# A mask added to attention scores by blocks of the identity: sixteen 32 by 32 products in place of four of 128 by 128

## The chip, the cores and the metric

The kernel runs on one core of one Trainium2 chip. The metric is the device time of one execution, in microseconds. A core has a matrix engine (TensorE, "PE" in the profile; its loading of the stationary operand stands apart as "PEld"), three engines for element-wise work (VectorE, "DVE"; ScalarE, "ACT"; GpSimd, "POOL"), and a queue engine that issues transfers ("SP"). Each engine works through its own instructions in order, and they wait for each other by semaphores.

## The reference: what is computed

One decoder layer over 128 sequences of 128 rows and 256 columns: self-attention, cross-attention against a context of the same size, and a feed-forward part with ternary weights, each behind a layer norm and added to its input. Attention has 16 heads of 16 columns. What the change touches is the mask in cross-attention:

```python
scores = jnp.einsum('bhqd,bhkd->bhqk', Q, K) / jnp.sqrt(jnp.float32(D_K))
scores = jnp.where(mask == 0, jnp.float32(1e-09), scores)
attn = jax.nn.softmax(scores, axis=-1)
```

One mask of 128 by 128 (query by key) serves all sequences and heads. A masked score is set to 1e-9, not to minus infinity.

## The kernel before

**Groups and steps.** Sequences are handled four at a time, in 32 groups. One step of attention is one sequence of one stage, all 16 heads. A period has eight steps: four of self-attention of a group and four of cross-attention of the group before it. So there are 128 steps of each stage.

**A step's scores are computed twice.** `maxima` forms scores with a query on each partition, only to find every row's largest value; `transposed_scores` forms them again with a key on each partition, which is what the later product with the values needs, and the maxima are brought in there. In `maxima`, four strips of 32 rows of the array work side by side (r = 0 to 3). The tiles s[0] and s[1] have two banks of PSUM each (a bank is 512 float32 per partition), so strip r has one bank, s[r // 2][:, r % 2], with four heads of 128 keys. In cross-attention the mask is added first: `ident_b`, the identity in bfloat16, times `never`, which is -1e30 where the mask is 0 and 0 elsewhere, repeated for four heads. That is one product per bank, over the whole 128 by 128 array (line 543). The products of queries and keys (line 554) then add to it. VectorE takes the maxima (`mx`, line 565).

**What frees what.** All score tiles, `s` and `st`, share four banks, so the first products of `maxima` wait until ScalarE's two exponentials (line 645) have read the step before. The transposed maxima `pn` (line 581) and the attention outputs `av` (line 657) share one more bank: `av` waits until `pn` has been read. In self-attention VectorE reads it for `q_max` (line 586); in cross-attention ScalarE reads it for `first` (line 596), and then VectorE reads both for `negm_t` (line 598).

**The order of a step**, as `attention` writes it by hand: the maxima of the following step; the outputs of the step before; the transposed scores of this step; the transposed maxima of the following one; in cross-attention, the weights of this step. Between these parts a string of letters, `ORDER`, says which piece of other work is put in: preparing self-attention (n), keys of the context (k), preparing cross-attention (c) and finishing a group with its feed-forward part (f). Nothing reorders the instructions later.

**The setup.** Before the first step the weights are loaded, one transfer after the other on SP's queue (line 153), then the mask (line 188). Two products per attention (line 177) take the value bias through the output weights. The mask is compared with 0 (`masked`, line 191) and scaled (`never`, line 193). Then comes the layer norm of the first group (lines 211 to 222), and its queries, keys and values, and then the ternary weights (lines 454 to 478), which load `raw` over the same queue.

**Buffers by tag.** Tiles of the pool `p_one` with one tag share one buffer. The tag `g_0` holds `bv_cols` of the setup, then `below`, and later a part of the feed-forward; `xn_0` and `xn_1` hold `unmasked` and `masked` in the setup.

The lines that the rest speaks of:

```python
    ident_b = const.tile([P, P], BF16, name="ident_b")
    nc.vector.tensor_copy(ident_b, ident)
...
            for r in range(S4):
                nc.tensor.matmul(
                    s[r // 2][:, r % 2],
                    ident_b,
                    never[:, None, :].to_broadcast([P, 4, P]),
                    start=True,
```

Of the kernel before, what the change touches and what calls it, by code (L numbers as in the profile page):

```python
# [18 lines left out]
F32 = mybir.dt.float32  # L19
F32R = mybir.dt.float32r  # L20
BF16 = mybir.dt.bfloat16
I32 = mybir.dt.int32
AF = mybir.ActivationFunctionType
ALU = mybir.AluOpType
AX = mybir.AxisListType
PSUM = bass.MemoryType.PSUM

P = 128
# [9 lines left out]
S4 = 4  # L38
# [3 lines left out]
NEVER = -1e30  # L42
# [17 lines left out]
def tile_decoder_layer(ctx: ExitStack, tc: tile.TileContext, a: dict, out: bass.AP):  # L60
    nc = tc.nc
    n_groups = a["x"].shape[0] // G

    const = ctx.enter_context(tc.tile_pool(name="const", bufs=1))
    p_in = ctx.enter_context(tc.tile_pool(name="p_in", bufs=5))
    p_act = ctx.enter_context(tc.tile_pool(name="p_act", bufs=2))
    p_one = ctx.enter_context(tc.tile_pool(name="p_one", bufs=1))
    p_att = ctx.enter_context(tc.tile_pool(name="p_att", bufs=2))
# [22 lines left out]

    ident = const.tile([P, P], F32, name="ident")
    make_identity(nc, ident)
    ident_b = const.tile([P, P], BF16, name="ident_b")
    nc.vector.tensor_copy(ident_b, ident)
    minus_half = const.tile([P, 1], F32, name="minus_half")
    nc.gpsimd.memset(minus_half, -0.5)
    masked_score = const.tile([P, 1], F32, name="masked_score")
# [7 lines left out]
        nc.vector.tensor_reduce(parity[:, e : e + 1], ident_heads[:, e], AX.XY, ALU.add)  # L106

    ident_strips = ident.rearrange("p (s r) -> p s r", s=S4)

# [2 lines left out]
    for n in range(4):  # L114
        for i in range(2):
            rows = ident_strips[:, :, 4 * i + n]
# [72 lines left out]

    masked = p_one.tile([P, P], F32, name="masked", tag="xn_1")  # L190
    nc.vector.tensor_scalar(masked, unmasked, 0.0, None, ALU.is_equal)
    never = const.tile([P, P], BF16, name="never")
    nc.vector.tensor_scalar(never, masked, NEVER, None, ALU.mult)

    least = const.tile([P, 1], F32, name="least")
    nc.vector.tensor_reduce(least, masked, AX.X, ALU.max)
# [336 lines left out]
    def score_tiles(name):  # L533
        return [ps_s.tile([P, 2, 4, P], F32, name=name, tag="s") for _ in range(2)]

    def maxima(stage, b, j):

        qt, kt = ready[stage, b]["q"], ready[stage, b]["k"]
        tok = slice(j * P, (j + 1) * P)
        s = score_tiles("s")  # L540
        if stage == "cross":
            for r in range(S4):
                nc.tensor.matmul(  # L543
                    s[r // 2][:, r % 2],
                    ident_b,
                    never[:, None, :].to_broadcast([P, 4, P]),
                    start=True,
                    stop=False,
                    skip_group_check=True,
                )  # L550
        for o in range(CC):
            for r in range(S4):
                strip = slice(r * 32, (r + 1) * 32)
                nc.tensor.matmul(  # L554
                    s[r // 2][:, r % 2, 2 * o : 2 * o + 2],
                    qt[strip, o, tok],
                    kt[strip, o, :, tok],
                    start=(stage == "self"),
                    stop=True,
                    skip_group_check=True,  # L560
                )

        mx = p_stat.tile([P, S4, 4, 2], F32, name="mx", tag="mx")[:, :, :, 0]
        for half in range(2):
            nc.vector.tensor_reduce(  # L565
                mx[:, 2 * half : 2 * half + 2], s[half], AX.X, ALU.max, negate=True
            )
        negm = negms[stage]
        if stage == "cross":
            twice = mx[:, :, None, :].to_broadcast([P, S4, 2, 4])  # L570
            nc.vector.tensor_scalar(negm[:, :, 0:2], twice, least, None, ALU.min)
        else:
            halves = negm.rearrange("p s a b -> p s (a b)").rearrange("p s (h d) -> p s h d", d=HD)
            heads = mx.rearrange("p s (o e) -> p s o e", e=2)
            for e in range(2):
                nc.vector.tensor_copy(halves[:, :, 1 - e, 0:CC], heads[:, :, :, e])
        return negm

    def transposed_maxima(stage, b, j, negm):
        pn = ps_av.tile([P, 4, P], F32, name="pn", tag="av")[:, 3]  # L580
        nc.tensor.transpose(pn, negm.rearrange("p s k n -> p (s k n)"), ident)  # L581
        if stage == "self":
            qt = ready[stage, b]["q"][:, :, j * P : (j + 1) * P]
            q_max = p_att.tile([P, CC, 2, P], F32, name="q_max", tag="q_max", bufs=1)
            for e in range(2):
                nc.vector.scalar_tensor_tensor(  # L586
                    q_max[:, :, e],
                    pn[:, None, :].to_broadcast([P, CC, P]),
                    max_rows[:, e : e + 1],
                    qt,  # L590
                    ALU.mult,
                    ALU.add,
                )
            return q_max
        first = p_att.tile([P, P], F32R, name="first", tag="first", bufs=1)
        nc.scalar.copy(first, pn)
        negm_t = p_att.tile([P, P], F32R, name="negm_t", tag="negm_t")
        nc.vector.scalar_tensor_tensor(
            negm_t, first.bitcast(F32), minus_second, pn, ALU.mult, ALU.add
        )  # L600
        return negm_t
# [70 lines left out]
    def attention():  # L672
        w_t = added = None
        for i in range(-1, 2 * G * (n_groups + 1) + 1):
            here, following, before = row(i), row(i + 1), row(i - 1)
            cross = i % (2 * G) >= G
            if following:
                negm = maxima(*following)
            if i >= 0:
                yield  # L680
            if before:
                outputs(*before, w_t)
            if i >= 0:
                yield
            if here:
                s = transposed_scores(*here, added)
                if not cross:
                    w_t = weights(here[0], s, None)
            if i >= 0:
                yield  # L690
            added_here = added
            if following:
                added = transposed_maxima(*following, negm)
            if i >= 0:
                yield
            if cross and i >= 0:
                if here:
                    w_t = weights(here[0], s, added_here)
                yield
# [76 lines left out]
```

## Time and profile before

| | |
|---|---|
| median of three runs | 2883.38 us (2882.04 to 2885.99) |
| the profiled execution | 2880.45 us, of it a span of 2878.4 us |
| granted clock of TensorE, mean over the span | 0.982 |
| scores for the maxima (line 554), TensorE busy | 299.0 us, 4096 records |
| outputs (line 657), TensorE busy | 279.1 us, 8192 records |
| maxima (line 565), VectorE | 512 of 1214 ns |
| exponentials (line 645), ScalarE | 512 of 1022 ns |

A float32 product leaves two records, one for each of its passes; bfloat16 and the rounded float32 form leave one. A record of TensorE gives the start of a product and a modelled end, which includes the time through the pipe, so consecutive products overlap in it; the start-to-start distance is what a product costs. The chain of waits goes back from the last instruction, at each step to what released it or to the instruction before it on its engine; its shares are shares of the span. In the groups, a name and an arrow read "written from read".

### The profile page before, as it was taken

The numbers are of one execution on the slowest core, as the hardware profiler recorded it, in microseconds if no ns is written. First come the engines' busy times: TensorE is split into PE (matmuls) and PEld (weight loads), VectorE is DVE, ScalarE is ACT, GpSimd is POOL, SyncE is SP. The second block draws the span as 40 slices with busy tenths as digits, with TensorE's granted clock in tenths as the row PEclk, the third lists the DMA queues.
The fourth block names the chain that finished last, engine by engine and source line by source line (L and its number), as shares of the span: only waits on it lengthen the run. The fifth ranks groups of instructions, "written<-read, shape, count | busy, mean of one in ns | idle before, by whom it ended". The sixth has DMA issues, their size and how long they took to land.

```text
span 2878.4 us, 73779 instructions
## 1 busy us (share of the span) xinstructions
PE 2768.6 (96%) x31261; PEld 1984.6 (69%) x31261; DVE 2048.5 (71%) x3787; ACT 1547.9 (54%) x2369; POOL 1373.5 (48%) x1425
## 2 busy tenths in 40 slices
PE   4789999999999999999999999999999999999985
PEld 2456777777777777777777767777777777777664
DVE  4467777777777777777777877777777777777663
ACT  0345555555555556555556555555655555555443
POOL 1324545454454545454455545454544545454343
PEclk8899999999999999999999999999999999999997
DMA  2111221121122122122112112211211221211101
GB/s 78 31 39 40 55 55 32 47 55 37 49 55 52 30 53 48 39 54 54 33 46 55 40 47 54 55 32 47 55 39 47 55 47 36 51 47 34 45 24 31
DMA packets 110359, 130.92 MB, mean 45 GB/s; under 512 B 32592, under 2 KB 68816, under 8 KB 110032
## 3 DMA queue, kind: packets, MB, share of 16 engines
q1 hardware_dynamic: 110032, 126.22, 17.8%
q8 instruction: 247, 4.05, 0.6%
q14 instruction: 80, 0.66, 0.1%
HBM read 71.65 MB, written 18.87 MB: 31 GB/s over the span
## 4 chain that ended last, share of the span: by engine, by line
PE 93%; DVE 3%; DMA 1%; POOL 1%; ACT 1%; issue 1%; SPq 0%; POOLq 0%; ACTq 0%; DVEq 0%
PE st L612 10%; PE s L554 10%; PE av L657 9%; PE py L431 9%; PE po L272 8%; PE ph L379 8%; PE pv L272 8%; PE pk L260 8%; PE pq L260 8%; PE pg L408 4%; PE s L543 4%; PE pt L240 3%; PE st L636 3%; PE pn L581 1%; DVE mx L565 1%; DVE st L622 1%
## 5 line engine op out<-in xcount | busy, mean ns | idle before, releaser
L565 DVE TENSOR_REDUCE mx<-s 128x8 f32<-128x1024 f32 x512 | 600.5, 1214 | 103.4 <-PE s L554 103.3
L217 POOL TENSOR_SCALAR rstd<-agg 128x4 f32<-128x4 f32 (+1 forms) x160 | 38.4, 240 | 1214.7 <-DVE agg L212 1214.7
L645 ACT ACTIVATE w_t<-st 128x1024 f32<-128x1024 f32 x512 | 496.4, 1022 | 225.0 <-PE st L612 196.8
L222 POOL TENSOR_SCALAR xn<-x,agg,rstd 128x256 f32<-128x256 f32 x384 | 465.5, 1225 | 10.0
L622 DVE COPY_PREDICATED_SCALAR st<-masked_t,masked_score 128x1024 f32 x256 | 315.7, 1279 | 85.4 <-PE st L612 82.6
L416 ACT ACTIVATE g<-pg,ln_w 128x256 fp32r<-128x256 f32 x512 | 211.9, 477 | 215.8 <-PE pg L408 212.6
L660 ACT COPY raw<-av 128x512 f32<-128x512 f32 x256 | 150.2, 587 | 318.8 <-PE av L657 318.5
L554 PE MATMUL s<-kt,qt 32*128 32x256 f32 x4096 | 299.0, 404 | 1.7 <-ACT w_t L645 1.7
L350 POOL TENSOR_TENSOR o_raw<-o_raw,factors 128x256 f32<-128x256 f32 x256 | 179.2, 728 | 243.0 <-DMA factors<-by_head 193.8
L657 PEld LDWEIGHTS av<-w_t,v 128*32 128x32 f32 x8192 | 209.7, 110 | 111.2 <-issue 44.8
L657 PE MATMUL av<-w_t,v 128*32 128x128 f32 x8192 | 279.1, 277 | 3.4 <-ACT w_t L645 1.2
L554 PEld LDWEIGHTS s<-kt,qt 32*128 32x128 f32 x4096 | 187.9, 186 | 132.9 <-issue 83.7
L222 POOL TENSOR_SCALAR g<-g,agg,rstd 128x1024 f32<-128x1024 f32 x64 | 276.3, 4317 | 6.7
L379 PE MATMUL ph<-w_fc,xn 128*128 128x512 f32 x1024 | 273.3, 409 | 1.2 <-ACT g L386 1.2
L431 PE MATMUL py<-w_proj,g 128*128 128x256 f32 x2048 | 271.2, 288 | 0.3 <-DVE g L418 0.3
L431 PEld LDWEIGHTS py<-w_proj,g 128*128 128x128 f32 x2048 | 254.2, 193 | 14.4 <-issue 9.6
L418 DVE SCALAR_TENSOR_TENSOR g<-pg,ln_w,g 128x256 fp32r<-128x256 f32 x512 | 216.7, 475 | 33.3 <-ACT g L416 29.8
L379 PEld LDWEIGHTS ph<-w_fc,xn 128*128 128x128 f32 x1024 | 188.0, 191 | 54.3 <-issue 16.4
L308 DVE COPY v<-pv 128x512 f32<-128x512 f32 x128 | 86.3, 674 | 147.6 <-PE pv L272 147.5
L586 DVE SCALAR_TENSOR_TENSOR q_max<-pn,max_rows,qt 128x256 f32<-128x256 f32 x256 | 110.5, 473 | 110.7 <-PE pn L581 110.7
L386 ACT ACTIVATE g<-ph 128x512 f32<-128x512 f32 x256 | 146.3, 597 | 78.9 <-PE ph L379 78.2
L354 DVE TENSOR_TENSOR x<-x,po 128x512 f32<-128x512 f32 x128 | 87.5, 683 | 110.2 <-PE po L272 110.2
(112 smaller groups left out, 4829.8 us busy)
## 6 DMA issues: line engine op xcount, KB each, us to landing
o_raw<-raw SPq DMA_DIRECT2D x512, 64.0 KB
factors<-by_head SPq DMA_DIRECT2D x128, 256.0 KB
x<-in_x_dram SPq DMA_DIRECT2D x32, 512.0 KB
ctx_t<-in_ctx_t_dram SPq DMA_DIRECT2D x32, 512.0 KB
out_dram<-x SPq DMA_DIRECT2D x32, 512.0 KB
sums<-raw SPq DMA_DIRECT2D x128, 16.0 KB
by_head<-r SPq DMA_DIRECT2D x64, 32.0 KB
raw<-in_w_fc_t_dram SPq DMA_DIRECT2D x1, 1024.0 KB
```

Source lines behind the costliest of these rows:

```text
L222: engine.tensor_scalar(dst[:, j], src[:, j], agg[:, j, 0:1], rstd[:, j : j + 1], ALU.subtract, ALU.mult)
L260: nc.tensor.matmul(out, w[:, c, o * P : (o + 1) * P], src_t[:, c], start=(c == 0), stop=(c == CC - 1))
L272: nc.tensor.matmul(rows[:, j], src_t[:, c, (j0 + j) * P : (j0 + j + 1) * P], w[:, c], start=(c == 0), stop=(c == CC - 1),)
L379: nc.tensor.matmul(ph, xn_parts[i][:, c, (j0 + j) * P : (j0 + j + 1) * P], w_fc[:, c, n * 512 : (n + 1) * 512], start=((i, c) == terms[0]) ...
L418: nc.vector.scalar_tensor_tensor(parts[1][:, f0 + f], pieces[:, f], scales[f], parts[0][:, f0 + f].bitcast(F32), ALU.mult, ALU.subtract,)
L431: nc.tensor.matmul(rows[:, j], parts[i][:, f, j * P : (j + 1) * P], w_proj[:, f], start=((i, f) == terms[0]), stop=((i, f) == terms[-1]),)
L554: nc.tensor.matmul(s[r // 2][:, r % 2, 2 * o : 2 * o + 2], qt[strip, o, tok], kt[strip, o, :, tok], start=(stage == "self"), stop=True, sk ...
L565: nc.vector.tensor_reduce(mx[:, 2 * half : 2 * half + 2], s[half], AX.X, ALU.max, negate=True)
L612: nc.tensor.matmul(s[r // 2][:, r % 2, n], kt[strip, n // 2, n % 2, tok], added[strip, n // 2, n % 2] if stage == "self" else qt[strip, n ...
L622: nc.vector.copy_predicated(s[half].rearrange("p r n q -> p (r n) q"), masked_t[:, None, :].to_broadcast([P, 8, P]), masked_score[:, :, No ...
L645: nc.scalar.activation(w_t[:, 2 * half : 2 * half + 2], s[half], AF.Exp)
L657: nc.tensor.matmul(av[32 * r : 32 * r + 32, n], v[:, j, head : head + 32], w_t[:, r, n], start=True, stop=True)
```

## The change

The mask is added by products of 32 by 32 blocks. The array's strip r and column group c take rows 32c to 32c + 31 of the queries for the four heads of bank r: the stationary operand is a 32 by 32 identity on the partitions of strip r, the moving operand is rows 32c to 32c + 31 of the mask, on those same partitions. So `ident_b` shrinks to four identities one below the other, and `never` becomes, on each strip, all 128 rows of the mask in four pieces of 32 rows. Four transfers lay the mask out that way in the setup (`rows`). The tile `first` takes the tag, and so the buffer, of `q_max`.

```diff
-    ident_b = const.tile([P, P], BF16, name="ident_b")
-    nc.vector.tensor_copy(ident_b, ident)
...
     ident_strips = ident.rearrange("p (s r) -> p s r", s=S4)
+    ident_32 = p_one.tile([P, 32], F32, name="ident_32", tag="g_0")
+    nc.vector.tensor_reduce(ident_32, ident_strips.rearrange("p s r -> p r s"), AX.X, ALU.add)
+    ident_b = const.tile([P, 32], BF16, name="ident_b")
+    nc.vector.tensor_copy(ident_b, ident_32)
...
-    never = const.tile([P, P], BF16, name="never")
-    nc.vector.tensor_scalar(never, masked, NEVER, None, ALU.mult)
+
+    rows = p_one.tile([P, S4, P], I32, name="rows", tag="g_0")
+    for r in range(S4):
+        nc.sync.dma_start(rows[r * 32 : (r + 1) * 32], a["mask"].rearrange("(c i) k -> i c k", c=S4))
+    never = const.tile([P, S4, P], BF16, name="never")
+    nc.vector.tensor_scalar(never, rows, 0.0, NEVER, ALU.is_equal, ALU.mult)
...
-            for r in range(S4):
-                nc.tensor.matmul(
-                    s[r // 2][:, r % 2],
-                    ident_b,
-                    never[:, None, :].to_broadcast([P, 4, P]),
-                    start=True,
-                    stop=False,
-                    skip_group_check=True,
-                )
+            for c in range(S4):
+                for r in range(S4):
+                    strip = slice(r * 32, (r + 1) * 32)
+                    nc.tensor.matmul(
+                        s[r // 2][c * 32 : (c + 1) * 32, r % 2],
+                        ident_b[strip],
+                        never[strip, c, None, :].to_broadcast([32, 4, P]),
+                        start=True,
+                        stop=False,
+                        skip_group_check=True,
+                    )
...
-        first = p_att.tile([P, P], F32R, name="first", tag="first", bufs=1)
+        first = p_att.tile([P, P], F32R, name="first", tag="q_max", bufs=1)
```

In the changed kernel the mask products are on line 551, the scores on 562, the transposed scores on 620 and the outputs on 665.

## The prediction

> **What bounds the kernel now.** I read the page first (busy shares, then the chain that ended last), then the groups by line and shape, then the chain over one period of 84.6 us in mid-run, then the timeline around the changed products, and last the chain of the first 70 us.
>
> ```profile
> span 2878.4 us, 73779 instructions
> ...
> PE 2768.6 (96%) x31261; PEld 1984.6 (69%) x31261; DVE 2048.5 (71%) x3787; ACT 1547.9 (54%) x2369; POOL 1373.5 (48%) x1425
> ...
> PE 93%; DVE 3%; DMA 1%; POOL 1%; ACT 1%; issue 1%; SPq 0%; POOLq 0%; ACTq 0%; DVEq 0%
> ...
> L543 PE MATMUL s<-never,ident_b 128*128 128x512 bf16 x512 | 133.9, 383 | 1.7 <-ACT w_t L645 1.6
> ```
>
> TensorE carries 93% of the chain, and the next engine is busy 71%. The changed line has 512 products, four in each of 128 steps of cross-attention. Their 133.9 us busy counts the pipe's tail, so I take the chain's pieces instead:
>
> ```profile
> 1412.09 0.11 PE pn L581
> 1412.20 0.86 PE s L543 x4
> 1413.06 1.08 PE s L554 x16
> 1414.13 1.01 PE av L657 x32
> ```
>
> Four products cost 0.86 us, 216 ns each, with nothing beside them. 128 times 0.864 is 110.6 us, 3.8% of the span. Now the starts inside (start, length, engine, line, what):
>
> ```profile
> 1412.03 1.03 PE L543 MATMUL s<-never,ident_b 128*128 128x512 bf16 x4
> 1412.73 0.87 DVE L586 SCALAR_TENSOR_TENSOR q_max<-pn,max_rows,qt 128x256 f32<-128x256 f32 x2
> 1412.99 0.74 PEld L554 LDWEIGHTS s<-kt,qt 32*128 32x128 f32 x16 [0.42 <-issue]
> ...
> 1412.68 0.38 PE L543 MATMUL s<-never,ident_b 128*128 128x512 bf16 x1
> ...
> 1413.74 0.39 PE L554 MATMUL s<-kt,qt 32*128 32x256 f32 x4
> ...
> 1414.06 0.14 PEld L657 LDWEIGHTS av<-w_t,v 128*32 128x32 f32 x5 [0.33 <-issue]
> ```
>
> The fourth product starts at 1412.68 and streams 0.213; the first load of the next form follows at 1412.99, 0.095 after the stream's end. The same 0.09 to 0.10 stands at every change of tile form I looked at. The four row-tiled products of one round (L554) finish within 0.39 of the first start though each takes 0.374: they start about 6.6 ns apart and run at once. The five column-tiled loads of L657 do so too: four 7 ns apart, the fifth, and with it the first product, 28 ns after the first load.
>
> **What the Trainium skill says.** "TensorE: Matmul & The Clock Gate", Part 3, measured speedup: sixteen 32 by 32 tiles with 512 columns ran 10.6 times as fast as one after the other, and a pack takes one product plus some 4 ns per further tile. The trace agrees for four row tiles and for four column tiles (3.3 to 6.6 ns apart); no line of it uses sixteen. That page's pack took 660 ns, so one product there took about 600 against 379 here: it says nothing on whether the faster stream is kept. "TensorEngine Tiling (Array Packing)", Key Properties: changing the tile form drains the array; here that is the 0.095. The same page, Gotcha 1: row tiles that run at once must write different banks. The new code gives strip r bank r, as L554 does.
>
> **The change part by part.**
>
> *Removed:* 0.864 us per step.
>
> *Added in its place, per step.* What stands before the four products is a 128 by 128 form in all 128 steps (63 after pn, the rest after lines 379, 260, 272 and 240), so today no drain stands there; the new form needs one: 0.095. The first load of 32 columns: 0.028, from L657 (for float32; bf16 cannot be much dearer). Sixteen starts: 15 gaps of 3.3 ns (L636, one pass) to 6.6 ns (L554), so 0.05 to 0.10, taken 0.075. The last stream: 0.213, as today. Sum 0.411. The drain ahead of L554 is there before and after. Saved: 0.864 - 0.411 = 0.453 us, between 0.43 and 0.48 by the gaps; times 128 = 58.0 us.
>
> *Can the instructions be fed?* 32 instructions stand where 8 did. Semaphore records of TensorE's sequencer stand 105 ns apart when adjacent and 165 with four products between, so one product costs it 15 ns and 32 some 0.5 us. In all 128 steps its last own wait before the mask products is over at least 1.8 us before they start, so I price this at nothing; if that lead were gone, the gaps would grow to some 30 ns and the step to 0.79.
>
> *First wait that takes some back.* The first and third old products wait for the two exponentials that free the score banks. With strips innermost, the third product comes not 0.43 after the first but 0.01.
>
> ```profile
> 1008.45 1.02 ACT L645 ACTIVATE w_t<-st 128x1024 f32<-128x1024 f32 x1
> ...
> 1009.21 1.03 PE L543 MATMUL s<-never,ident_b 128*128 128x512 bf16 x4
> ```
>
> Here the second exponential ends at 1009.47, 0.26 after the first product's start, plus 0.04 to wake (what waiting products show). The new third product would be ready at 0.095 + 0.028 + 0.01 = 0.13: it waits 0.17 to 0.18, and everything on TensorE's queue behind it too (the other tiles, L554, av). I compared all 128 steps: 30 look like this one (one per period), five near the ends are later still by some 0.3; in the rest the second exponential is over. 30 x 0.18 + 5 x 0.3 = 6.9 us back.
>
> *Second.* Once per period pn of a self step stands right ahead of the mask products, and av (L657) right behind the scores. av's bank is pn's, and q_max frees it. Above, q_max ends at 1413.60 and av's first load starts at 1414.06, 0.46 later; such a hand-over takes about 0.16 (an av that waits starts 0.106 after its semaphore record, which takes 0.05 after the update). So 0.30 is to spare, and 0.453 is wanted: 0.15 x 31 = 4.7 us back. q_max itself waits for VectorE's copy of v, not for the scores, so it doesn't come earlier. The other three av of a period, the transposed scores behind mx, and line 636 behind the predicated copy have either more to spare or move along with the scores; I allow 1 us for them.
>
> *Prologue.* never, today on 128 x 128 behind masked, now reads rows, which four new DMAs fill; they stand on SP between the mask's load and the load of w_fc (SP's issues, then the chain).
>
> ```profile
> 12.56 1.58 SPq L188 DMA_DIRECT2D unmasked<-in_mask_dram  x1
> 15.82 0.37 SPq L454 DMA_DIRECT2D raw<-in_w_fc_t_dram  x1
> ...
> 13.72 2.09 PE pb L177 x4
> ...
> 16.43 0.23 DVE never L193
> ...
> 17.48 0.35 DVE stats L211
> ...
> 21.19 4.86 POOL xn L222 x4
> 26.09 1.33 PE pt L240 x5
> ```
>
> rows takes the buffer that a product of pb frees, as the w_fc load at 15.82 does (its buffer by the other product): the first issue falls between 14.9 and 15.8, the fourth three issue slots of 0.51 later, at 16.4 to 17.4. From issue to use took 2.6 us for the first sums, and at most 3.6 for the mask itself; I take 2.0 to 3.5. So never starts at 18.4 to 20.9 instead of 16.43, and lasts some 0.35 longer for four times the elements (by line 222 on VectorE, 0.82 for 1024). least and stats stand behind it on VectorE, and xn, the transposes and the first projections behind stats: 2.3 to 4.8 us, taken 3.5, all on the chain. w_fc's load comes four slots (2 us) later, but is read only at 40.8. ident_32, its sum and its small copy lie in VectorE's wait of 1.97 us for the first biases.
>
> *At nothing:* first now shares q_max's buffer. first is written after pn, which TensorE runs after the last scores that read q_max; q_max is written by VectorE after the operation that reads first. Neither gains a wait; if one did, it would be at two of eight steps. One semaphore record more on ScalarE and two on VectorE are all that the program shows.
>
> *Sum:* -58.0 + 6.9 + 4.7 + 1.0 + 3.5 = -41.9 us. The profiled execution took 2880.45 (span 2878.4 and 2.05 around it), so 2838.6; the median of the runs is 2883.38, 2.9 higher, so 2841.5, as I forecast: 2842.
>
> **The rivals.**
>
> *A. The tiles run together, but at half the stream rate.* For: sixteen tiles[...] write four banks in each column group; L554 and L657 are float32 at half that rate, and L636, the one-pass row-tiled line, starts a round only every 0.11 us, though its stream of 128 columns would take 0.053. Against: those rounds are as long as a load of 128 columns (0.107), which explains them. Then 0.213 becomes 0.427, a step 0.625, saved 30.6; the exponential's wait stays, q_max's falls away: -30.6 + 6.9 + 3.5 = -20.2, so 2863.
>
> *B. Only four tiles run at once: slower.* No line has tiles of one strip and different column groups in flight on different data together with other strips. If the next group of four waits for the strip, the place is L551 itself: 0.095 + 0.028 + 4 x 0.216 = 0.987, 0.123 more per step, 15.7 in all; with 6.9 and 3.5 it is +26, so 2909. It decides once starts and streams together last over 0.66 us, just over three rounds. Against it: the skill's 10.6, and the overlapping loads and products of L657.
>
> *C. The gain turns into waits.* VectorE's 71% are dense where four steps follow each other. If, beside q_max, the other three hand-overs of a period fell short by about as much (0.15 x 96 = 14 us), the result would be 2856. Against: the idle time that TensorE shows before av now is small.
>
> *D. The change does something else:* excluded; the program has sixteen loads and sixteen products on sixteen tile positions per step.
>
> **How the numbers follow.** My forecast 0.70, A 0.14, B 0.09, C 0.07. Its own range is 2833 (gaps of 3.3 ns, short prologue, half of the waits) to 2852. The range of 2830 to 2868 takes in C and A and leaves out B and the tails. About 0.2% (5.8 us) is what a measurement can tell. Faster: all of the first, A and C but a few hundredths: 0.88; same: 0.03; slower: B, 0.09.
>
> **What would show it.** Right: sixteen products of L551 start within 0.1 us of each other; the piece on the chain is about 0.4 us with the drain, and L562 starts 0.31 after the last start; idle time before L551 by w_t of 5 to 8 us, before av by q_max of about 5; stats starts near 21 us. Wrong: last starts 0.43 apart from the next form's load plus 0.095 (A), starts in four groups 0.2 apart (B), idle time before av in all steps (C), or a prologue that is later by more than 5 us.

## The result, and the profile after

| | before | after |
|---|---|---|
| median of five runs each | 2885.99 us | 2839.25 us |
| lowest to highest | 2882.04 to 2887.87 | 2837.91 to 2845.54 |
| ratio after to before | | 0.9844, 95% interval 0.983 to 0.9859 |

The ratio stands for 45 us, between 41 and 49; the two medians are 46.7 apart. The forecast took 41.9 us off the median then known, 2883.38, which gave 2842.

The profiled execution of the changed kernel was the slowest of its five, 2845.54 us; the one shown of before, 2880.45, was below all five of its runs in the table. So these two executions are only 35 us apart. The page (span; busy time by engine; chain by engine and line) and the group of the changed line (operation, shapes, count; busy us and mean ns; idle time before):

```profile
span 2843.5 us, 76860 instructions
...
PE 2723.7 (96%) x32797; PEld 1965.4 (69%) x32797; DVE 2045.6 (72%) x3788; ACT 1546.9 (54%) x2369; POOL 1371.8 (48%) x1425
...
PE 93%; DVE 3%; DMA 1%; POOL 1%; issue 1%; ACT 1%; SPq 0%; POOLq 0%; ACTq 0%; DVEq 0%
```

```profile
L551 PE MATMUL s<-never,ident_b 32*32 32x512 bf16 x2048 | 64.8, 388 | 2.8 <-ACT w_t L653 2.7
```

The bound is what it was: TensorE has 93% of the chain. 2048 products stand where 512 stood, each as long in the records (388 ns against 383), and together they are busy for 64.8 us instead of 133.9. That is only possible if they lie beside each other. The chain of the changed kernel through the first two cross steps of a period in mid-run (start, us, engine, what, line, records):

```profile
1398.32 0.11 PE pn L589
1398.43 0.36 PE s L551 x16
1398.80 1.15 PE s L562 x16
1399.94 0.04 issue
1399.98 1.08 PE av L665 x32
...
1406.87 0.11 PE pn L589
1406.98 0.36 PE s L551 x16
1407.34 1.08 PE s L562 x16
1408.42 1.91 PE pq L266 x4
1410.33 1.01 PE av L665 x32
1411.35 1.24 PE st L620 x30
```

The mask now takes 0.36 us where it took 0.86. Three places give some of it back. In the first step the scores and av take 1.15 and 1.08 with 0.04 between, where 1.08 and 1.01 stood: av waits. In the second step the transposed scores take 1.24 where they took 1.10. This is that step in the chain of before:

```profile
1421.07 0.86 PE s L543 x4
1421.93 1.07 PE s L554 x16
...
1425.93 1.10 PE st L612 x32
```

And in the third cross step the mask itself takes longer. There the timeline of the changed kernel has this (start, length of the run of records, engine, line):

```profile
1417.02 1.02 ACT L653 ACTIVATE w_t<-st 128x1024 f32<-128x1024 f32 x1
...
1417.88 0.64 PE L551 MATMUL s<-never,ident_b 32*32 32x512 bf16 x16
```

The exponential ends at 1418.04, 0.16 after the first product; the sixteen take 0.64 with their tails here against 0.43 in the other steps, because the third of them starts 0.21 us after the first and not 0.007. So the saving of 4 x 0.50 us per period became 1.43: from the first mask product of a group to that of the next it was 84.61 us before and is 83.18, within 0.02 us in every period of the middle. The 31 distances from the first group to the last add up to 43.0 us less (2601.0 and 2558.0).

Ahead of that, the first mask product came 7.3 us later than in the profile of before, 2.8 of it by the first scores (71.2 against 68.4 us). The first experiment looks at this.

### The profile page after: what moved, and what is told of

It reads as the page before. It is cut to its first block, busy times and chain, and to the rows that moved or that the text cites. A ratio compares the mean times of both kernels' runs of the same rounds, so it can differ in the third digit from the quotient of the medians.

```text
span 2843.5 us, 76860 instructions
## 1 busy us (share of the span) xinstructions
PE 2723.7 (96%) x32797; PEld 1965.4 (69%) x32797; DVE 2045.6 (72%) x3788; ACT 1546.9 (54%) x2369; POOL 1371.8 (48%) x1425
## 4 chain that ended last, share of the span: by engine, by line
PE 93%; DVE 3%; DMA 1%; POOL 1%; issue 1%; ACT 1%; SPq 0%; POOLq 0%; ACTq 0%; DVEq 0%
PE st L620 10%; PE s L562 10%; PE av L665 9%; PE py L437 9%; PE po L278 9%; PE ph L385 8%; PE pv L278 8%; PE pq L266 8%; PE pk L266 8%; PE pg L414 4%; PE pt L246 3%; PE st L644 3%; PE s L551 2%; PE pn L589 1%; DVE mx L573 1%
```

## The experiments

"Period" is the median distance between the first mask products of two groups. All times stand beside runs of the kernel before on the same chip, whose medians were 2885.2 to 2886.3 us.

**1. The changed kernel again.**

> The changed kernel once more, beside the runs of the others. In its first profile the steady period lasted 83.18 us against 84.61 before (1.43 less, 44 us in 31 periods), but the first mask product came 7.3 us later than before, 2.8 of it in the setup and 4.5 in the filling that follows, where one transfer of factors took 6.7 us instead of 3.7 and the clock was low longer. Theory: the 4.5 us are chance of that execution. Then a second profile has the same 83.18 us period, and the first mask product 2 to 4 us later than before. Rival: the change itself delays the filling; then the 7 us return. Time: 2836 to 2846.

Measured: 2840.31 us (2839.82 to 2845.43), ratio 0.9851 (0.9836 to 0.9865); period 83.17; the first statistics at 21.0 us, the first scores at 70.7 and the first mask product at 157.5, 5.5 later than in the first profile of before. The period repeats to 0.01 us. But the first mask product came later than the theory's 2 to 4 us, and earlier than the rival's 7, so this run alone does not decide. All thirteen profiles tell more. Here is the filling, the stretch from the first scores to the first mask product, beside the mean granted clock of TensorE over it:

| filling, us | mean granted clock | kernels |
|---|---|---|
| 83.2 to 84.1 | 0.84 to 0.85 | before, runs 3 and 4 |
| 85.2 to 85.5 | 0.81 | runs 10 and 11 |
| 86.8 to 88.2 | 0.80 to 0.83 | the changed kernel, runs 1, 2, 5, 6, 7 and 8 |
| 90.7 | 0.77 | run 9 |

On the whole the filling is longer where the granted clock was lower. Kernels with the old setup (before, runs 5, 10 and 11) and with the new one have both short and long fillings, so a longer filling is not shown to come from the change. But three of the four with the old setup are in the upper two rows and only two of the nine with the new one, so it is not excluded either: why the clock differed from one execution to the next is not shown.

**2. never filled later.**

```diff
-    rows = p_one.tile([P, S4, P], I32, name="rows", tag="g_0")
-    for r in range(S4):
-        nc.sync.dma_start(rows[r * 32 : (r + 1) * 32], a["mask"].rearrange("(c i) k -> i c k", c=S4))
...
-    nc.vector.tensor_scalar(never, rows, 0.0, NEVER, ALU.is_equal, ALU.mult)
...
     run_now(ternary_weights())
+    rows = p_one.tile([P, S4, P], I32, name="rows", tag="g_0")
...
+    nc.vector.tensor_scalar(never, rows, 0.0, NEVER, ALU.is_equal, ALU.mult)
```

> The changed kernel with the four transfers of rows and never moved behind the ternary weights. Theory: VectorE's wait for rows holds up the layer norm of the first group by 2.6 us, and that is the whole cost of the setup. Then the first statistics start at 17.5 us as before and not at 20.0, the first scores at 68.5 instead of 71.3, and the time is 2 to 3 us lower than the changed kernel's. Rival: the setup is held up by the queue's four more issues, wherever they stand; then the first scores still come after 70 us, and the time stays.

Measured: 2841.46 us (2838.76 to 2844.32), ratio 0.9848 (0.9831 to 0.9865); first statistics at 18.3, first scores at 69.4, first mask product at 157.4. Both starts moved forward, by 1.7 and 1.8 us against the first profile and 2.7 and 1.3 against the second; but the time is the same within its spread, and the first mask product came at the same time too. So the wait for rows holds up the setup by some 2 us, near the 2.6 expected; that this counts in the time is not shown.

**3. The mask added twice.** The second set adds to the first, so the mask's value is doubled and the output unchanged by it.

```diff
-            for c in range(S4):
+            for again, c in [(0, c) for c in range(S4)] + [(1, c) for c in range(S4)]:
...
-                        start=True,
+                        start=not again,
```

> The changed kernel with the sixteen mask products made twice, the second time added to the first (the mask's value doubles, masked scores are still far below every other). Theory: sixteen products that run at once cost one stream of 0.213 us and a few ns each, so a second set costs 0.22 to 0.24 us per step, 28 to 31 us in all, less what the steps that wait for an exponential hide (30 of them 0.21 at most): 22 to 31 us over the changed kernel. Rival 1, the feed of instructions is what a set costs (32 instructions of 15 ns): 0.48 per step, 55 to 62 us. Rival 2, half of the stream rate: 0.43 per step, 50 to 55 us.

Measured: 2860.5 us (2856.93 to 2864.11), 20 over the run beside it. The same first step, from the chain of this kernel:

```profile
1403.17 0.11 PE pn L589
1403.28 0.58 PE s L551 x32
1403.86 1.08 PE s L562 x16
1404.94 1.01 PE av L665 x32
```

A second set costs 0.58 - 0.36 = 0.22 us: one stream. Its first product starts 0.226 after the first set's first, the sixteen again within 0.05. Both rivals fall. And the period grew by 0.51, not by 4 x 0.22: scores and av are back at 1.08 and 1.01 here with no gap. The two hand-overs that the short mask left waiting (0.18 and 0.14 per period) absorb most of the difference. The expectation lacked these two. It let the steps that wait for an exponential hide a part instead, and they hide nothing: in the third cross step too the second set adds 0.22. Hence 20 and not 22 or more.

**4. pn in another bank.**

```diff
-        pn = ps_av.tile([P, 4, P], F32, name="pn", tag="av")[:, 3]
+        pn = bank("pn")[:, 0:P]
```

> The changed kernel with pn in a bank of the three that rotate, not in the one of av. Theory: once per period av waits 0.18 us for q_max, which reads pn from that bank; with another bank the wait goes, and a period falls from 83.18 to about 83.0 us, 5 us in all. Rival: the rotating banks are the scarcer thing; pn holds one of them for 1 to 2 us in every step, and products of the other parts wait for it instead: the period grows by 0.2 us or more, and the time by 6 us or more.

Measured: 2854.49 us (2849.67 to 2857.03), period 83.51. Two parts of its chain:

```profile
1396.97 0.36 PE s L551 x16
1397.33 1.07 PE s L562 x16
1398.41 1.01 PE av L665 x32
...
1451.43 0.45 PE pg L414 x4
...
1452.83 0.89 DVE g L424 x2
1453.71 0.14 issue
1453.85 0.63 PE pg L414 x4
```

Both theories hold, each at its place, and the rival's loss is the larger. av no longer waits (1.07 and 1.01). But pg, transposes of the feed-forward part that stand behind a pn of self-attention, need a rotating bank. At 1453.85 they start only when VectorE has read the bank of the pg before (g, line 424). The list of TensorE's waits has 31 of pg for this g here, 8.7 us, against 2 in the changed kernel, 2.3 us. From one pg to the next it is 2.58 us here and 2.20 there: 0.38 of the loss. Another 0.13 falls on transposes behind the copies of the keys (pt, line 246). pn itself does not wait there for a bank; the expectation of run 8 reads that place wrongly. The net is a loss of 0.33 per period.

**5. Column tiles alone, on the kernel before.**

```diff
             for r in range(S4):
-                nc.tensor.matmul(
-                    s[r // 2][:, r % 2],
-                    ident_b,
+                for c in range(S4):
+                    nc.tensor.matmul(
+                        s[r // 2][c * 32 : (c + 1) * 32, r % 2],
+                        ident_b[:, c * 32 : (c + 1) * 32],
...
```

> The kernel before, with its identity and its mask as they were, but each of the four products cut into four column tiles of 128 by 32, bank after bank: sixteen products again, of which only the four of one bank can run at once. Theory: the gain comes from sixteen tiles at once, so here nothing is gained and the change of form is added: a step takes 0.095 + 0.03 + 4 x 0.216 = 0.99 us against 0.864, 0.12 more, 0.5 per period: 85.1 us, and 2895 to 2905 in all, slower than before. Rival: small tiles, short loads or the order of issue are what helps; then a period falls below 84.6.

Measured: 2897.74 us (2891.86 to 2898.62), ratio 1.0032 (1.0019 to 1.0045): slower. Period 85.05. The chain:

```profile
1422.96 0.11 PE pn L582
1423.07 0.98 PE s L544 x16
1424.05 1.08 PE s L555 x16
```

Sixteen small products take 0.98 us when four at a time can run (starts at 0, 0.226, 0.441 and 0.657), and 0.36 when sixteen can. So narrow tiles with short loads bring nothing by themselves; what counts is how many run at once. This is what the forecast's slower rival would have looked like, without the exponential's wait.

**6. and 7. Scores in the same tiles.** In the first of the two for cross-attention (cols are 32 queries), in the second, with `parts = S4`, for self-attention too.

```diff
+        parts = S4 if stage == "cross" else 1
         for o in range(CC):
-            for r in range(S4):
...
+            for c in range(parts):
+                for r in range(S4):
...
+                    cols = slice(c * P // parts, (c + 1) * P // parts)
...
+                        s[r // 2][cols, r % 2, 2 * o : 2 * o + 2],
+                        qt[strip, o, j * P : (j + 1) * P][:, cols],
...
```

> The changed kernel with the scores of cross-attention (not of self-attention) cut into the same 32 by 32 tiles as the mask, 32 products for 8. Theory: between mask and scores stand the drain of 0.095 and a first load of 128 columns of 0.108; in one form the drain goes and the load falls to 0.03, while later starts within a round add up to 0.1: 0.1 to 0.17 us less per step in three of the four cross steps, nothing in the one that waits for q_max and mx: a period of 82.7 to 82.9 us, 2823 to 2832 in all. Rival 1: float32 products of strips and column groups together don't all run at once; then scores take twice as long or more, and a period over 86 us. Rival 2: the feed of 64 more records per step isn't hidden; then starts in a step stand 15 to 30 ns apart and the period grows by 1 to 3 us.

> As the run with one form, and the scores of self-attention in 32 by 32 tiles as well, where no drain is saved, since another form stands ahead either way. Theory: the short first load (0.08 less) and the spread of starts (0.05 to 0.1 more) cancel: within 0.1 us per period of the run with one form in cross-attention alone. If the load is what counts and not the drain, the period falls by another 0.3; if the starts count more, it grows by 0.3 or more.

Measured: 2868.47 us (2868.05 to 2869.71), period 83.87; and 2912.5 us (2908.71 to 2914.47), period 85.26. The theory was wrong. From the chain of the first:

```profile
1443.40 0.36 PE s L551 x16
1443.77 1.34 PE s L565 x53
```

The drain did go: the scores' first load stands 2 ns behind the start of the last mask product, not 0.31 us, and their first product 0.23 us behind the first mask product, not 0.36. But the scores take 1.34 us instead of 1.08. The first eight start within 0.03 us; from then on many of the starts lie some 17 ns apart, in runs of eight, and 64 records spread over 1.17 us. That is the spacing of the second rival, though its period is smaller than it said. So sixteen float32 tiles didn't start as closely as the sixteen of bfloat16 did. Whether TensorE's feed or the number of float32 products that can be open at once sets this, these runs don't tell. With self-attention in the same tiles another 1.39 is lost where no change was expected: the starts count, not the first load.

**8. One pn in another bank.**

```diff
+        if stage == "self" and j == G - 1:
+            pn = bank("pn")[:, 0:P]
+        else:
+            pn = ps_av.tile([P, 4, P], F32, name="pn", tag="av")[:, 3]
```

> The changed kernel with pn in a rotating bank in one step of eight alone, the self step whose pn stands ahead of the first mask of a period. In the run with pn always there, av's wait for q_max went as foretold, but pn waited elsewhere for a bank that the copies of the keys still held, and a period grew from 83.18 to 83.51 us. Theory: where only this pn moves, the gain of 0.15 to 0.2 stays and the loss goes: a period of 83.0 us and 5 us less in all (2835). Rival: the bank is missed here too (products of v and of the queries stand around it); then 83.2 or more.

Measured: 2837.01 us (2836.57 to 2838.55), ratio 0.9827 (0.9811 to 0.9844), period 83.00.

```profile
1395.80 0.11 PE pn L592
1395.91 0.36 PE s L551 x16
1396.28 1.08 PE s L562 x16
1397.35 1.01 PE av L668 x32
```

av's wait is gone (1.08 and 1.01, no gap), and nothing waits for the bank elsewhere: 0.18 less per period, some 5.5 us over 31 of them. Of the kernels run, this has the lowest time; the interval of its ratio overlaps that of the changed kernel, so it is the period that shows the gain.

**9. Loops exchanged.**

```diff
-            for c in range(S4):
-                for r in range(S4):
+            for r in range(S4):
+                for c in range(S4):
```

> The changed kernel with the loops over strips and column groups exchanged: all four column groups of strip 0 first. Theory: all sixteen tiles are independent, so the order doesn't matter to a step of 0.36 us, and the product that waits for the second exponential is the ninth, not the third, which is 0.02 us later: a period of 83.15 to 83.2 us, 2836 to 2846 in all. Rival: a load for a strip waits while that strip streams, and only the order in which the strips change hides it; then starts of one strip stand 0.03 us or more apart, a step grows by 0.1 or more, a period by 0.4.

Measured: 2845.27 us (2844.37 to 2847.4), period 83.15. All sixteen start within 0.05 us here too, and in the third step the first eight do, while the ninth comes 0.21 after the first. The order of the tiles doesn't matter to the step; what waits is the bank. The time is 5 us over run 1 and lies outside the steady part: the first mask product came at 161.2 us, 3.6 later than there, and the mean granted clock of the filling was the lowest of all profiles, 0.77 (table under run 1). Whether the order of the loops has a part in that is not shown.

**10. and 11. Two edits on the kernel before.** In 10 `first` takes the tag q_max; in 11 the one pn of run 8 takes a rotating bank.

> The kernel before with nothing changed but the buffer of first, which is that of q_max. Theory: no wait is added, in no step: a period of 84.61 us as before, 2879 to 2890 in all. Rival: writing first waits for the scores that read q_max, or q_max for the reader of first; then the period grows by 0.1 us or more.

> The kernel before with the one pn ahead of a period's first mask in a rotating bank, the edit that took 0.18 us per period off the changed kernel. Theory: before, av had some 0.3 us to spare behind q_max, and the wait arose only with the shorter mask products; so here the edit brings nothing: a period of 84.6 us, 2880 to 2890 in all. Rival: the edit helps for a reason of its own; then the period falls here too, by 0.1 to 0.2 us.

Measured: 2886.18 us, ratio 1.0 (0.9991 to 1.0009), and 2885.82 us, ratio 1.0001 (0.9993 to 1.001); both periods 84.61. The shared buffer costs nothing. And the edit that takes 0.18 us off a period of the changed kernel takes nothing off the old one: the change made av's wait for q_max.

## Why the prediction was right, point by point

- **Sixteen at once, at the full rate.** Right. The starts lie 3.3 ns apart, the stream and the drain behind it take 0.313 after the last start, and a second set costs one stream (run 3). Rival A, half the rate, would have shown 0.53 there. Run 5 has what rival B supposed, four tiles at once, though in tiles of 128 by 32, and costs what B's sum says, less the exponential's wait.
- **The step.** From the end of the stream ahead to the first load of the scores the forecast has the drain ahead, the mask and the drain behind, 0.411 + 0.095 = 0.506; measured is 0.459. The drain ahead was exact: the first product starts 0.202 after pn's, which streams 0.107. Two terms were too large: the first load was priced at 0.028 and takes about 0.005, and the gaps at 5 ns are 3.3. Before, the same stretch took 0.957. So 0.498 us is saved per step and not 0.453: 5.8 us more in all, the largest error of the sum, and on the safe side.
- **The feed.** Right: no step of the middle shows gaps wider than 4 ns, except in the steps with the wait below.
- **The exponential's wait.** Right in place, and nearly in number: 29 steps of the middle for the 30 foretold, 0.21 us for 0.18, and seven steps near the ends for five. Together 8.2 us in the first profile, for 6.9.
- **av behind q_max.** Right: 0.18 for 0.15, in the first cross step of each period, and runs 8 and 11 show that this is its cause and that it is new.
- **Other hand-overs.** Too low, the term sized worst: I allowed 1 us in all. In the second cross step the transposed scores lose 0.14 us per period, 4.3 us in 31. The timeline of the changed kernel there, VectorE and TensorE:

```profile
1408.27 0.39 DVE L217 BATCH_NORM_STATS2 stats<-x 128x6 f32<-128x256 f32 x1
1408.69 0.18 DVE L218 BATCH_NORM_AGGREGATE agg<-stats 128x2 f32<-128x6 f32 x1
1408.79 0.32 DVE L606 SCALAR_TENSOR_TENSOR negm_t<-first,minus_second,pn 128x128 fp32r<-128x128 f32 x1
1409.02 2.35 DVE L573 TENSOR_REDUCE mx<-s 128x8 f32<-128x1024 f32 x2
...
1411.28 1.31 PE L620 MATMUL st<-qt,kt 32*128 32x128 f32 x32
```

VectorE takes the maxima right behind the statistics and negm_t, until 1411.37; the transposed scores start at 1411.28 and wait there for the second pair of banks: the third of them starts 0.145 after the second, where 0.007 is usual. I had written that these hand-overs would move along with the scores; but the scores end at 1408.42 in the chain and this read starts when VectorE is free of other work, 0.6 later.
- **The setup.** About right: foretold 3.5 us. In the four profiles with the old setup (before, runs 5, 10 and 11) the first statistics start at 17.4 to 18.0 us and the first scores at 68.0 to 68.8. In the eight with the new one (all others but run 2) they start at 19.9 to 21.6 and 70.0 to 72.2, on average 3.2 and 2.7 later. In the first profile the issue of rows started at 15.4 and never at 18.8. Whether this shows in the time is left open by run 2.
- **The signs.** Those read from starts came. The two idle times did not: 2.7 us before line 551 by w_t, where 5 to 8 were foretold, and 1.1 before av by q_max, for about 5. Both waits fall while earlier products are still in the pipe and count as busy, so they show in the distance between starts and not as idle time.
- **The shared buffer.** Right (run 10).
- **The sum.** Per period 4 x 0.498 - 0.21 - 0.18 - 0.14 = 1.46, and 1.43 is measured. With the measured sizes the forecast's own sum reads -63.7 + 8.2 + 5.6 + 4.3 + 2.7 = -42.9 us (tiles, exponential, q_max, other hand-overs, setup), for the -41.9 foretold. That lies within the 41 to 49 us of the result. The mechanism was right but for the transposed scores behind the maxima, and that the total came so close was luck: 5.8 us too little of gain and 5.5 too little of waits nearly cancel.

## What to carry to other kernels

A product with the identity as its stationary operand wastes twelve of the sixteen blocks of 32 by 32, those off the diagonal. Here four such products were cut into sixteen, each with its own pair of strip and column group and each strip with its own bank, and all sixteen cost one stream in place of four, plus one drain for the change of form. When such a piece gets shorter, ask of every wait behind it whether its releaser starts with the shortened piece or with something else: those that start with something else (q_max behind a copy, the maxima behind statistics, the exponentials) take back what they lack in slack. Before counting on more, try the same cut on the next product: here the float32 products in the same tiles got slower, not faster.

## What the runs showed of the hardware that I had not expected

- In 32 by 32 tiles the products of bfloat16 start 3.3 ns apart, sixteen within 0.05 us; those of float32, with two records each, start that closely only for the first eight, and then many of them some 17 ns apart (run 6: 1.34 us for scores that take 1.08 in strips of 32 by 128).
- A first load of 32 columns in bfloat16 delays its product by about 0.005 us (records of 384 ns, against 379 in the old form); in float32, on line 657 of before, it was 0.025 to 0.028 (first records of 297 ns, later ones of 272).
- Between bfloat16 and float32 products in the same tiles no drain stands (run 6): 2 ns from the start of the last product to the next load, against 0.31 with a change of form, which is the stream of 0.213 and the drain of 0.095.
- The granted clock ahead of the first mask product differed between executions, from 0.77 to 0.85 in the mean of the filling, and the filling took 90.7 to 83.2 us with it.
